# Three changes of buffers in a two-layer decoder: weight pieces loaded a step ahead, projection input placed in the V tiles, query and key stacks as half tiles

## The chip, the cores and the metric

The kernel runs on one core of one Trainium2 chip. The metric is device time in microseconds (us) for one execution of the whole program. A core has five engines with instruction queues of their own: TensorE (PE, matmuls and transposes; its weight loads are listed as PEld), VectorE (DVE), ScalarE (ACT), GpSimd (POOL) and SyncE (SP), which in this kernel issues the DMA transfers. An engine executes its instructions in the order of its queue; between engines, semaphores hold an instruction back until what it needs is there.

## What is computed

The input x has 4 sequences of 1024 tokens and 256 channels, and there is a context of 77 tokens for each sequence. Two pre-LayerNorm layers with residuals follow one another, all in float32:

```
x = x + L0_attn (layernorm(x))            # 16 heads of 16, causal softmax with ALiBi, projection
x = x + L0_xattn(layernorm(x), ctx)       # 16 heads of 64 over the 77 context tokens
x = x + L0_ffn  (layernorm(x))            # BitLinear: silu(gate) * up, then down, inner width 1024
x = x + L1_attn (layernorm(x))            # 16 heads of 16, causal, power attention
x = x + L1_xattn(layernorm(x), ctx)       # 8 heads of 64
x = x + L1_ffn  (layernorm(x))            # FP4: silu(gate) * up, then down, inner width 704
```

The power attention takes weights exp(Z - max Z) with Z = 2 log(|q.k| + 1e-7) + log(scale) + G[t] - G[s], where G is the running sum of log-sigmoid gates that come from 16 extra columns of the same projection. BitLinear rounds weights to three values and activations to 8 bits. The FP4 feed forward rounds weights and activations to the E2M1 grid (0, 0.5, 1, 1.5, 2, 3, 4, 6) with one scale per block of 16 values:

```
scale = max(max|block| / 6, 1e-12)
q     = grid[searchsorted(midpoints, |block / scale|)] * sign * scale
```

## The kernel before

**Precision.** Float32 products are made from a high and a low part of each operand: `split_sb` (ACT copies the high part at L179, DVE subtracts it at L180) and `mm3` (three matmuls, L191). Queries and keys of the attentions are held as three bfloat16 parts, which are laid on top of each other as rows of one contraction.

**Stages.** Sequences are called batches, b = 0 to 3. In phase 0 the layer-0 attention of batch b, `A0(b)`, is the main stream, and the layer-0 cross attention and feed forward of batch b - 1 (`XA(b-1,0)`, `F0(b-1)`) are the side stream; preparations of weights go beside them (`prep_x`, `prep_a1`, `prep_f1_up` beside batch 2, `prep_f1_down` beside batch 3). In phase 1 the layer-1 attention `A1` is the main stream and `XF` (the layer-1 cross attention and feed forward `F1` of the batch before) the side stream; the first side stream is `F0(3)` with what goes before it. After the last main step a tail remains, the cross attention and the feed forward of batch 3, where `F1` runs in several lanes at once, each with its own set of borrowed buffers (the table `FL`, L137 to L142).

**Order.** The streams are Python generators that `weave` and `zip2` interleave by step counts. The framework then orders each engine's instructions by a planner and gives each tile a buffer of its tag. `BUFS` (L128) says how many buffers a tag has; tags that are not listed have one. A tile of a tag has to wait until the last reader of the tile that had the buffer before is done, and its load is then held on SyncE, with whatever is queued behind it. A DMA's issue also waits for the DMA eight issues before it to be complete. PSUM banks are handed out in turn (`BANKS`).

**The front of an attention.** `qkv` (L262 to L307) does a batch in two halves of 512 tokens. `ln` (L215) takes a tile, loads x into it (L223), and normalises: statistics on DVE (L200, L202), a few small steps on GpSimd, and L226 on GpSimd. In phase 0 this tile has the tag "X" (four buffers, shared with the residual's tiles of `load_x`, L167); in phase 1 it is the tag "xn" with one buffer, which the cross attention and the feed forwards use too. A "V" tile is taken next and its padding and its columns of ones are written by GpSimd (L276, L277). The normalised half is transposed by TensorE (L235, tag "Q"), split, multiplied by the weights for queries and keys (results split into bfloat16 parts, L290 to L293, and written to DRAM `dr`, L296 and L297), and for values, which ACT writes into the V tile (L304).

**Stacks.** `stacks` (L310 to L327) brings the parts of four heads back from DRAM: QS by L323 with four DMAs (two sets of parts, two halves of 512 tokens), KS by L320 with two, and in layer 0 the ALiBi rows by L325 and L326. QS and KS have two buffers each, for all 1024 tokens. In layer 0, `a0_max` computes scores on TensorE (L352, and the mask by L356) whose row maxima DVE takes (L357); the negative maxima go back into two rows of QS as a DMA (L386, from a tile VsJ); then `a0_main` multiplies keys by queries again (L401, L403), ACT exponentiates (L404), and TensorE multiplies by V (L413). The next group's `a0_max` is woven with the present group's `a0_main`. In layer 1 the scores are L901, DVE takes them at L907, ACT at L909, GpSimd at L912, and the product with V is L930.

**Weights of the last feed forward.** `prep_f1_up` (L1022 to L1041) does four pieces (w_gate and w_up, two each): it loads a piece into a "wst" tile (two buffers, which all weight preparations share, L1029), rounds it to FP4 in two parts by `fp4` (DVE L1008 to L1011, GpSimd L1012, ACT L1014, DVE L1015 and L1016, GpSimd L1017), transposes it (L1036), splits it and writes it to DRAM `g1d` (L1040). `prep_f1_down` does w_down in two pieces likewise (load L1048, write L1059).

```
    BUFS = {"X": 4, "V": 4, "QS": 2, "KS": 2, "P": 4, "ot": 2, ... "VsJ": 4, "wst": 2, ...}
        for half in range(2):
            xn = self.ln(None, half, src, alt={"xn": "X"} if self.phase == 0 else None)
            V.append(self.t([128, 4, H * 17 + 15], F32, "V"))
```

Of the kernel before, what the change touches and what calls it, by code (L numbers as in the profile page):

```python
# [12 lines left out]
F32 = mybir.dt.float32  # L13
F32R = mybir.dt.float32r
BF = mybir.dt.bfloat16
# [7 lines left out]
B, T, C = 4, 1024, 256  # L23
# [67 lines left out]
class Kern:  # L91
# [13 lines left out]
    def __init__(self, ctx, tc, ins, out, consts, nb=B):  # L105
# [21 lines left out]

    BUFS = {"X": 4, "V": 4, "QS": 2, "KS": 2, "P": 4, "ot": 2, "q4s": 2, "qr": 2, "VsJ": 4, "wst": 2, "E": 2, "kh": 1, "qp": 2, "g_ew": 2}  # L128

# [9 lines left out]
        {"xn": "ot", "xX": "QS", "E": "V", "xph": "y0", "xpl": "y1", "wst": "P", "kh": "KS", "q4s": "VsJ", "ps": 0},  # L139
        {"xn": "DL0", "xX": "QS", "E": "V", "xph": "WAh", "xpl": "WAl", "wst": "P", "kh": "yTh", "q4s": "VsJ", "ps": 1},  # L140
        {"xn": "DL1", "xX": "KS", "E": "V", "xph": "qp", "xpl": "qp", "wst": "P", "kh": "yTl", "q4s": "VsJ", "ps": 1},
    )  # L142
# [72 lines left out]
    def ln(self, b, g, src=None, t0=0, n=4, alt=None):  # L215

        nc = self.nc
        xn = self.t([128, n if alt else 4, C], F32, "xn", alt)[:, :n]
        if src is None:
            x = self.X[b, g][:, t0 : t0 + n]  # L220
        else:
            x = xn
            nc.sync.dma_start(x, src.rearrange("(g t p) c -> g p t c", g=2, p=128)[g])  # L223
# [40 lines left out]
    def qkv(self, src, wd, nw, gl=None, w=None):  # L264
# [7 lines left out]
        for half in range(2):  # L272
            xn = self.ln(None, half, src, alt={"xn": "X"} if self.phase == 0 else None)
            V.append(self.t([128, 4, H * 17 + 15], F32, "V"))
            vv.append(V[half][:, :, 0 : H * 17].rearrange("p t (h e) -> p t h e", e=17))
            nc.gpsimd.memset(V[half][:, :, H * 17 :], 0.0)  # L276
            nc.gpsimd.memset(vv[half][:, :, :, 16:17], 1.0)  # L277
            h = self.t([128, 2, 512], F32R, "yTh")
            l = self.t([128, 2, 512], F32R, "yTl")
            self.xT(xn, h, l, "Q")  # L280
# [29 lines left out]
    def stacks(self, g, dr, alibi):  # L310

        nc = self.nc
        QS = self.t([110, 2, 4, 512], BF, "QS")
        KS = self.t([110, 4, T], BF, "KS")
        c, o = g // 2, (g % 2) * 4
        for st, t0 in ((QS, (1, 0)), (KS, (4, 5))):
            for r in range(2):
                v = dr[c][t0[r] : t0[r] + 3].rearrange("t (d h) n -> (t d) h n", h=8)[:, o : o + 4, :]
                if st is KS:
                    nc.sync.dma_start(KS[r * 48 : r * 48 + 48], v)  # L320
                else:
                    for a in range(2):
                        nc.sync.dma_start(QS[r * 48 : r * 48 + 48, a], v[:, :, a * 512 : a * 512 + 512])  # L323
# [1005 lines left out]
```

## Time and profile before

| | |
|---|---|
| median of three runs | 2400.75 us (2393.45 to 2407.63) |
| the profiled execution | 2399.32 us, of which 2397.5 us are the span of the profile |
| mean granted TensorE clock | 0.953 of full speed |
| TensorE busy | 2149.5 us (90%) |
| VectorE / ScalarE / GpSimd busy | 1698.9 (71%) / 1637.4 (68%) / 1195.4 us (50%) |
| DMA | 238.45 MB in 182,697 packets, mean 99 GB/s |

The shares of busy time are means over stages with different limits, so single stretches are looked at as well. A line of the windows view gives, for a stretch, its length, then the busy time and the number of instructions in brackets of TensorE, weight loads, VectorE, ScalarE and GpSimd, then the granted clock, the share of the DMA engines' time that was used, and the rate in GB/s. A line of the waits view names the engine, the tile and line of the waiting instruction, after the arrow what released it, and then the total, the number and the longest of these waits. The chain of waits follows the work that ended last back through what released it; each piece has its start, its length and what it was.

### The profile page before, as it was taken

What the parts mean: (1) busy time and instruction counts of PE and PEld (TensorE: products, weight loads), DVE (VectorE), ACT (ScalarE), POOL (GpSimd) and SP (SyncE); (2) the same over time, 40 slices, a digit from 0 to 9 for tenths busy, and PEclk for the clock granted to TensorE, in tenths of its full rate; (3) what the DMA queues carried; (4) which work ended last, traced back from release to release, by engine and by line L of the source; (5) the groups of instructions that cost most, each with busy time, mean ns of one, the idle gap of its engine ahead of it and who ended that gap; (6) DMA issues with size and microseconds to landing.
All of it is one profiled execution on the core that took longest, in us unless ns stands there. A gap on an engine that the chain in (4) does not pass through costs nothing.

```text
span 2397.5 us, 51455 instructions
## 1 busy us (share of the span) xinstructions
PE 2149.5 (90%) x19110; PEld 1522.7 (64%) x19110; DVE 1698.9 (71%) x3781; ACT 1637.4 (68%) x4173; POOL 1195.4 (50%) x1942
## 2 busy tenths in 40 slices
PE   6898999998999998999989988899988998898886
PEld 5564557755667754676546765567766776676676
DVE  4776457677766787775756677778767786777776
ACT  4474456676756675665768978887678777888542
POOL 7322212254231442412545457777767787876664
PEclk9898899999999999899989999999999999999897
DMA  8975321223841337312252224412331224442000
GB/s 257 286 193 168 101 72 44 73 64 105 265 105 44 86 95 196 87 44 58 87 174 52 67 70 147 128 39 74 92 104 38 56 88 121 92 98 71 10 10 18
DMA packets 182697, 238.45 MB, mean 99 GB/s; under 512 B 16198, under 2 KB 165846, under 8 KB 175958
## 3 DMA queue, kind: packets, MB, share of 16 engines
q1 hardware_dynamic: 182446, 235.15, 35.5%
q8 instruction: 151, 2.47, 0.4%
q14 instruction: 100, 0.82, 0.1%
HBM read 152.62 MB, written 82.21 MB: 98 GB/s over the span
## 4 chain that ended last, share of the span: by engine, by line
PE 64%; DVE 13%; ACT 8%; DMA 7%; POOL 5%; issue 2%; SPq 1%; DVEq 0%; ACTq 0%; POOLq 0%
PE T L191 11%; PE W L191 9%; PE O L413 7%; PE Q L191 6%; PE O L930 6%; PE S L401 5%; PE M L352 5%; PE S L901 4%; DVE P L907 2%; DVE s_mt L357 2%; PE T L726 2%; PE W L633 1%; ACT P L909 1%; DMA KS<-c_alk 1%; PE M L356 1%
## 5 line engine op out<-in xcount | busy, mean ns | idle before, releaser
L357 DVE TENSOR_REDUCE s_mt<-M 128x1 f32<-128x512 f32 (+3 forms) x608 | 386.1, 655 | 103.9 <-PE M L356 76.2
L404 ACT ACTIVATE P<-S 128x512 f32<-128x512 f32 (+1 forms) x640 | 340.2, 563 | 149.4 <-PE S L401 93.0
L909 ACT ACTIVATE P<-P,eps 128x1024 f32<-128x1024 f32 x320 | 344.6, 1084 | 55.1 <-DVE P L907 52.5
L907 DVE TENSOR_REDUCE P<-S 128x512 f32<-128x512 f32 (+1 forms) x480 | 285.7, 611 | 83.9 <-PE S L901 61.8
L352 PE MATMUL M<-KS,QS 108*128 108x512 bf16 (+3 forms) x768 | 225.6, 339 | 43.3 <-DVE s_mt L357 27.5
L901 PE MATMUL S<-QS,KS 96*128 96x256 bf16 (+1 forms) x1280 | 219.0, 269 | 42.0 <-DVE P L907 35.9
L191 PE MATMUL T<-R,xX 128*128 128x352 f32 (+1 forms) x1136 | 246.8, 332 | 4.9 <-ACT E L622 1.9
L401 PE MATMUL S<-QS,KS 110*128 110x256 bf16 (+1 forms) x1280 | 230.7, 268 | 15.6 <-ACT P L404 8.0
L625 POOL TENSOR_TENSOR E<-E,s_xsm 128x616 f32<-128x616 f32 x64 | 77.8, 1217 | 316.9 <-DVE s_xsm L623 188.3
L413 PE MATMUL O<-P,V 128*32 128x256 f32 (+1 forms) x2560 | 231.4, 374 | 0.1
L191 PEld LDWEIGHTS T<-R,xX 128*128 128x128 f32 x1136 | 183.0, 190 | 25.6 <-ACT E L622 6.5
L912 POOL TENSOR_TENSOR P<-P,y 128x512 f32<-128x512 f32 x128 | 166.5, 1309 | 48.3 <-ACT P L909 28.1
L191 PE MATMUL W<-R,xph 128*128 128x256 f32 (+1 forms) x952 | 184.9, 292 | 3.3 <-ACT xph L179 2.6
L622 ACT ACTIVATE E<-T,s_xmx 128x77 f32<-128x77 f32 x512 | 159.4, 334 | 25.7 <-DVE s_xmx L619 23.0
L930 PE MATMUL O<-P,VsJ 128*32 128x128 f32 x3584 | 171.4, 286 | 5.6 <-ACT P L909 5.3
L901 PEld LDWEIGHTS <-KS 96*128 96x128 bf16 x1280 | 103.9, 99 | 113.4 <-issue 90.6
L401 PEld LDWEIGHTS <-KS 110*128 110x128 bf16 x1280 | 106.4, 100 | 104.9 <-issue 57.2
L191 PEld LDWEIGHTS W<-R,xph 128*128 128x128 f32 (+1 forms) x952 | 149.9, 192 | 12.1 <-issue 3.6
L352 PEld LDWEIGHTS <-QS 108*128 108x128 bf16 x768 | 68.1, 99 | 116.0 <-issue 88.2
L191 PE MATMUL W<-R,xpl 128*128 128x256 f32 (+2 forms) x476 | 139.1, 292 | 1.4 <-DVE xpl L180 1.2
L179 ACT ACTIVATE xph<-W 128x512 fp32r<-128x512 f32 (+2 forms) x180 | 79.6, 459 | 86.6 <-PE W L636 39.6
L733 POOL TENSOR_TENSOR R<-wst 128x256 f32<-128x256 f32 x128 | 92.4, 732 | 83.0 <-DVE wst L732 71.2
(353 smaller groups left out, 5683.8 us busy)
## 6 DMA issues: line engine op xcount, KB each, us to landing
QS<-dr SPq DMA_DIRECT2D x144, 192.0 KB
KS<-dr SPq DMA_DIRECT2D x72, 384.0 KB
dr<-qp SPq DMA_DIRECT2D x32, 768.0 KB
MD<-R SPq DMA_DIRECT2D x24, 616.0 KB
UD<-R SPq DMA_DIRECT2D x24, 512.0 KB
R<-MD SPq DMA_DIRECT2D x32, 308.0 KB
X<-in_x SPq DMA_DIRECT2D x16, 512.0 KB
dr<-qp SPq DMA_DIRECT2D x32, 256.0 KB
```

Source lines behind the costliest of these rows:

```text
L191: nc.tensor.matmul(out, x, y, start=first and n == 0, stop=last and n == len(seq) - 1)
L352: nc.tensor.matmul(Sv[:, x, 0:w], QS[:108, i // 4, hh, i % 4 * 128 : i % 4 * 128 + 128], KS[:108, hh, k0:k1], start=x == 0, stop=not diag ...
L357: nc.vector.tensor_reduce(out, Sv[:, :, 0:w], AX.X, ALU.max)
L401: nc.tensor.matmul(S[:, e, 0:w], st[1][:110, hh, j * 128 : (j + 1) * 128], st[0][:110, q0 // 512, hh, q0 % 512 : q0 % 512 + w], start=e == ...
L404: nc.scalar.activation(P[:, 2 * p : 2 * p + 2, 256 - w :], S[:, :, 0:w], AF.Exp)
L413: nc.tensor.matmul(O[0][hh * 32 : hh * 32 + 32, o + o0 : o + 256], V[j // 4][:, j % 4, h * 17 : h * 17 + 32], P[:, hh, o0:], start=c % 2 = ...
L622: nc.scalar.activation(E[:, n * 77 : (n + 1) * 77], Sv[:, k, :], AF.Exp, bias=mx[:, n : n + 1], accum_out=sm[:, n : n + 1])
L901: nc.tensor.matmul(S[:, e, 0:w], st[r][1][:96, hh, j * 128 : (j + 1) * 128], st[r][0][:96, q0 // 512, hh, q0 % 512 : q0 % 512 + w], start= ...
L907: nc.vector.tensor_reduce(Pv, S[:, :, 0:w].unsqueeze(3), AX.X, ALU.max, apply_absolute_value=True)
L909: nc.scalar.activation(Pw, Pw, AF.Square, bias=self.eps1)
L912: nc.gpsimd.tensor_tensor(Pd, Pd, Ds[r, c][:, j - 2 * c], ALU.mult)
L930: nc.tensor.matmul(Oc[rows, o0 : o0 + 128], lhs, P[:, hh, c0 : c0 + 128], start=j == 2 * c and i == 2 * c, stop=fin and i == 2 * c + 1)
```

## The change

The change has three parts. The computing instructions stay the same in number and shape on every engine.

1. In `prep_f1_up` each piece's load is issued before the piece ahead of it is rounded. The pieces go alternately into a tile of the tag "DU" and one of "wst". In `prep_f1_down` both pieces are loaded at the start.
2. In `qkv`, the two halves of x are loaded straight into the two V tiles at the start of the front, and `ln` normalises them there in place. The writing of V's padding and ones goes behind the transposes that read the normalised values. No "X" or "xn" tile is taken for it any more.
3. `stacks` makes four tiles, QS0, QS1, KS0 and KS1, each with 512 tokens and with two buffers of its own, and loads QS0 and KS0 first, each with its ALiBi rows, then QS1 and KS1. A stack of layer 0 takes 12 DMAs (8 before), one of layer 1 takes 8 (6 before). The users pick the half by the token, and the borrowed buffers of `FL` get the new tags.

```diff
@@ -125,7 +125,7 @@
         self.w1 = None
         self.drn = 0
 
-    BUFS = {"X": 4, "V": 4, "QS": 2, "KS": 2, "P": 4, "ot": 2, "q4s": 2, "qr": 2, "VsJ": 4, "wst": 2, "E": 2, "kh": 1, "qp": 2, "g_ew": 2}
+    BUFS = {"X": 4, "V": 4, "QS0": 2, "QS1": 2, "KS0": 2, "KS1": 2, "P": 4, "ot": 2, "q4s": 2, "qr": 2, "VsJ": 4, "wst": 2, "E": 2, "kh": 1, "qp": 2, "g_ew": 2}
 
 
     BANKS = (
@@ -136,9 +136,9 @@
     XL = {"xX": "yTh", "R2": "yTl", "M0": "WAh", "M1": "WAl", "U0": "qp", "U1": "qp", "E": "V", "xph": "qr", "xpl": "qr"}
     FL = (
         None,
-        {"xn": "ot", "xX": "QS", "E": "V", "xph": "y0", "xpl": "y1", "wst": "P", "kh": "KS", "q4s": "VsJ", "ps": 0},
-        {"xn": "DL0", "xX": "QS", "E": "V", "xph": "WAh", "xpl": "WAl", "wst": "P", "kh": "yTh", "q4s": "VsJ", "ps": 1},
-        {"xn": "DL1", "xX": "KS", "E": "V", "xph": "qp", "xpl": "qp", "wst": "P", "kh": "yTl", "q4s": "VsJ", "ps": 1},
+        {"xn": "ot", "xX": "QS0", "E": "V", "xph": "y0", "xpl": "y1", "wst": "P", "kh": "KS0", "q4s": "VsJ", "ps": 0},
+        {"xn": "DL0", "xX": "QS1", "E": "V", "xph": "WAh", "xpl": "WAl", "wst": "P", "kh": "yTh", "q4s": "VsJ", "ps": 1},
+        {"xn": "DL1", "xX": "KS1", "E": "V", "xph": "qp", "xpl": "qp", "wst": "P", "kh": "yTl", "q4s": "VsJ", "ps": 1},
     )
 
     @staticmethod
@@ -215,12 +215,11 @@
     def ln(self, b, g, src=None, t0=0, n=4, alt=None):
 
         nc = self.nc
-        xn = self.t([128, n if alt else 4, C], F32, "xn", alt)[:, :n]
         if src is None:
+            xn = self.t([128, n if alt else 4, C], F32, "xn", alt)[:, :n]
             x = self.X[b, g][:, t0 : t0 + n]
         else:
-            x = xn
-            nc.sync.dma_start(x, src.rearrange("(g t p) c -> g p t c", g=2, p=128)[g])
+            x = xn = src
         rs, mb = self.stats(x)
         for i in range(n):
             nc.gpsimd.tensor_scalar(xn[:, i, :], x[:, i, :], mb[:, i : i + 1], rs[:, i : i + 1], ALU.add, ALU.mult)
@@ -270,14 +269,16 @@
             self.n += 1
             dr.append(self.dr.tile([8, 128, T], BF, tag=f"dr{c}", name=f"dr{c}_{self.n}", bufs=2))
         for half in range(2):
-            xn = self.ln(None, half, src, alt={"xn": "X"} if self.phase == 0 else None)
             V.append(self.t([128, 4, H * 17 + 15], F32, "V"))
+            nc.sync.dma_start(V[half][:, :, :C], src.rearrange("(g t p) c -> g p t c", g=2, p=128)[half])
+        for half in range(2):
+            xn = self.ln(None, half, V[half][:, :, :C])
+            h = self.t([128, 2, 512], F32R, "yTh")
+            l = self.t([128, 2, 512], F32R, "yTl")
+            self.xT(xn, h, l, "Q")
             vv.append(V[half][:, :, 0 : H * 17].rearrange("p t (h e) -> p t h e", e=17))
             nc.gpsimd.memset(V[half][:, :, H * 17 :], 0.0)
             nc.gpsimd.memset(vv[half][:, :, :, 16:17], 1.0)
-            h = self.t([128, 2, 512], F32R, "yTh")
-            l = self.t([128, 2, 512], F32R, "yTl")
-            self.xT(xn, h, l, "Q")
             yield
             hs = slice(half * 512, (half + 1) * 512)
             for c in range(2):
@@ -310,20 +311,19 @@
     def stacks(self, g, dr, alibi):
 
         nc = self.nc
-        QS = self.t([110, 2, 4, 512], BF, "QS")
-        KS = self.t([110, 4, T], BF, "KS")
+        QS, KS = [], []
         c, o = g // 2, (g % 2) * 4
-        for st, t0 in ((QS, (1, 0)), (KS, (4, 5))):
-            for r in range(2):
-                v = dr[c][t0[r] : t0[r] + 3].rearrange("t (d h) n -> (t d) h n", h=8)[:, o : o + 4, :]
-                if st is KS:
-                    nc.sync.dma_start(KS[r * 48 : r * 48 + 48], v)
-                else:
-                    for a in range(2):
-                        nc.sync.dma_start(QS[r * 48 : r * 48 + 48, a], v[:, :, a * 512 : a * 512 + 512])
-        if alibi:
-            nc.sync.dma_start(QS[96:108], self.c["alq"][:, g])
-            nc.sync.dma_start(KS[96:110], self.c["alk"][:, g * 4 : g * 4 + 4, :])
+        for a in range(2):
+            n = slice(a * 512, a * 512 + 512)
+            for st, nm, t0 in ((QS, "QS", (1, 0)), (KS, "KS", (4, 5))):
+                t = self.t([110, 4, 512], BF, f"{nm}{a}")
+                st.append(t)
+                for r in range(2):
+                    v = dr[c][t0[r] : t0[r] + 3].rearrange("t (d h) n -> (t d) h n", h=8)[:, o : o + 4, n]
+                    nc.sync.dma_start(t[r * 48 : r * 48 + 48], v)
+            if alibi:
+                nc.sync.dma_start(QS[a][96:108], self.c["alq"][:, g, a])
+                nc.sync.dma_start(KS[a][96:110], self.c["alk"][:, g * 4 : g * 4 + 4, n])
         return QS, KS
 
 
@@ -349,7 +349,7 @@
             st_ = 512 // n
             Sv = S.rearrange("p (n k) -> p n k", n=n)
             for x, (hh, i, k0, k1) in enumerate(pieces):
-                nc.tensor.matmul(Sv[:, x, 0:w], QS[:108, i // 4, hh, i % 4 * 128 : i % 4 * 128 + 128], KS[:108, hh, k0:k1], start=x == 0, stop=not diag and x == n - 1)
+                nc.tensor.matmul(Sv[:, x, 0:w], QS[i // 4][:108, hh, i % 4 * 128 : i % 4 * 128 + 128], KS[k0 // 512][:108, hh, k0 % 512 : k0 % 512 + w], start=x == 0, stop=not diag and x == n - 1)
             if diag:
                 r = self.maskb if n == 1 else self.maskb.unsqueeze(1).to_broadcast([128, n, 128])
                 o = Sv[:, 0, w - 128 : w] if n == 1 else Sv[:, :, w - 128 : w]
@@ -383,7 +383,7 @@
         nc.scalar.activation(pr[:, 0, :], ps[:16, :128], AF.Copy)
         nc.vector.tensor_tensor(pr[:, 1, :], ps[:16, :128], pr[:, 0, :], ALU.subtract)
         for p in range(2):
-            nc.sync.dma_start(st[0][108 + p : 109 + p, part].rearrange("o h (i n) -> o (h i) n", n=128), pr[:, p, :])
+            nc.sync.dma_start(st[0][part][108 + p : 109 + p].rearrange("o h (i n) -> o (h i) n", n=128), pr[:, p, :])
 
     def a0_main(self, st, V, y, g, O, pend):
         nc = self.nc
@@ -398,7 +398,7 @@
                 S = self.p("S").rearrange("p (h k) -> p h k", h=2)
                 for e in range(2):
                     hh = 2 * p + e
-                    nc.tensor.matmul(S[:, e, 0:w], st[1][:110, hh, j * 128 : (j + 1) * 128], st[0][:110, q0 // 512, hh, q0 % 512 : q0 % 512 + w], start=e == 0, stop=not dg and e == 1)
+                    nc.tensor.matmul(S[:, e, 0:w], st[1][j // 4][:110, hh, j % 4 * 128 : j % 4 * 128 + 128], st[0][q0 // 512][:110, hh, q0 % 512 : q0 % 512 + w], start=e == 0, stop=not dg and e == 1)
                 if dg:
                     nc.tensor.matmul(S[:, :, 0:128], self.identb, self.maskTb.unsqueeze(1).to_broadcast([128, 2, 128]), start=False, stop=True)
                 nc.scalar.activation(P[:, 2 * p : 2 * p + 2, 256 - w :], S[:, :, 0:w], AF.Exp)
@@ -898,7 +898,7 @@
                 S = self.p("S").rearrange("p (h k) -> p h k", h=2)
                 for e in range(2):
                     hh = 2 * p + e
-                    nc.tensor.matmul(S[:, e, 0:w], st[r][1][:96, hh, j * 128 : (j + 1) * 128], st[r][0][:96, q0 // 512, hh, q0 % 512 : q0 % 512 + w], start=e == 0, stop=e == 1)
+                    nc.tensor.matmul(S[:, e, 0:w], st[r][1][j // 4][:96, hh, j % 4 * 128 : j % 4 * 128 + 128], st[r][0][q0 // 512][:96, hh, q0 % 512 : q0 % 512 + w], start=e == 0, stop=e == 1)
                 Pv = P[:, 2 * p : 2 * p + 2, 256 - w :]
                 self.absn += 1
                 if self.absn % 8 in ABS_ACT:
@@ -1022,11 +1022,19 @@
     def prep_f1_up(self):
         nc = self.nc
         self.g1d = self.dr.tile([2, 128, 2, 2, 2, 352], F32, name="g1d")
-        for n, nm in enumerate(("w_gate", "w_up")):
-            src = self.i["L1_ffn_" + nm].rearrange("(t p) k -> p t k", p=88)
+        sts = []
+
+        def load(n, t2):
+            src = self.i["L1_ffn_" + ("w_gate", "w_up")[n]].rearrange("(t p) k -> p t k", p=88)
+            sts.append(self.t([128, 1024], F32, "DU" if t2 == 0 else "wst")[:88])
+            nc.sync.dma_start(sts[-1].rearrange("p (t k) -> p t k", k=256), src[:, t2 * 4 : t2 * 4 + 4, :])
+
+        load(0, 0)
+        for n in range(2):
             for t2 in range(2):
-                st = self.t([128, 1024], F32, "wst")[:88]
-                nc.sync.dma_start(st.rearrange("p (t k) -> p t k", k=256), src[:, t2 * 4 : t2 * 4 + 4, :])
+                st = sts.pop()
+                if (n, t2) != (1, 1):
+                    load(n + t2, 1 - t2)
                 for k in range(2):
                     self.fp4(st[:, k * 512 : (k + 1) * 512], 32, 1e-12)
                 yield
@@ -1043,9 +1051,12 @@
     def prep_f1_down(self):
         nc = self.nc
         self.d1d = self.dr.tile([128, 2, 6, 256], F32, name="d1d")
+        sts = []
         for r in range(2):
-            st = self.t([128, 1024], F32, "wst")[:, :704]
-            nc.sync.dma_start(st[:, 0:704], self.i["L1_ffn_w_down"][r * 128 : (r + 1) * 128, :])
+            sts.append(self.t([128, 1024], F32, "wst")[:, :704])
+            nc.sync.dma_start(sts[r], self.i["L1_ffn_w_down"][r * 128 : (r + 1) * 128, :])
+        for r in range(2):
+            st = sts[r]
             self.fp4(st[:, 0:704], 44, 1e-12)
             for c2 in range(3):
                 ps = self.p("T")
```

## The prediction

> **What bounds the kernel now.** I read the shares of the engines first, then the windows, the waits of each engine, and the chain of waits around the places that the diff touches.
>
> ```profile
> span 2397.5 us, 51455 instructions
> ...
> PE 2149.5 (90%) x19110; PEld 1522.7 (64%) x19110; DVE 1698.9 (71%) x3781; ACT 1637.4 (68%) x4173; POOL 1195.4 (50%) x1942
> ...
> PE 64%; DVE 13%; ACT 8%; DMA 7%; POOL 5%; issue 2%; SPq 1%; DVEq 0%; ACTq 0%; POOLq 0%
> ```
>
> TensorE is the bound, and it is idle for 2397.5 - 2149.5 = 248 us. The change has the same compute instructions on every engine (the two programs' counts agree), so it can only move idle time and clock. The profiled run took 2399.3 us, 1.4 below the median of 2400.75; the sum is made against 2399.3.
>
> Windows by stage (columns: PE, weight loads, DVE, ACT, POOL busy, granted clock, DMA share, GB/s):
>
> ```profile
> 60.00:120.00 60.00, 49.29 (x270) 33.09 (x270) 45.35 (x84) 26.19 (x60) 18.75 (x17) 0.86 0.95 287
> ...
> 900.00:960.00 60.00, 48.43 (x391) 24.20 (x390) 43.92 (x94) 33.10 (x64) 12.85 (x18) 0.91 0.74 196
> ```
> ```profile
> 170.00:180.00 10.00, 5.42 (x49) 3.52 (x48) 6.04 (x12) 4.08 (x9) 0.00 (x0) 0.86 1.05 230
> 180.00:190.00 10.00, 8.75 (x74) 4.89 (x75) 5.58 (x14) 4.16 (x9) 3.72 (x3) 0.80 0.82 255
> 190.00:200.00 10.00, 6.61 (x27) 2.77 (x26) 5.46 (x10) 1.68 (x3) 1.12 (x2) 0.55 1.01 336
> ```
> ```profile
> 2200.00:2245.30 45.30, 40.66 (x496) 27.56 (x496) 36.19 (x77) 35.44 (x52) 28.57 (x51) 0.96 0.04 14
> 2245.30:2397.50 152.20, 114.75 (x710) 105.66 (x710) 101.92 (x201) 56.55 (x163) 89.36 (x104) 0.85 0.03 11
> ```
>
> TensorE has its holes where a stack of queries and keys or a weight arrives late (170 to 200, 900 to 960), with a lower granted clock behind each hole, and in the tail behind the last L901, which starts at 2245.3. Waits of TensorE, then of VectorE (total us, times, longest):
>
> ```profile
> PE M L352 <- DMA KS<-c_alk: 6.4, 4, 2.6
> ...
> PE M L352 <- DMA MD<-R: 5.2, 1, 5.2
> ```
> ```profile
> DVE q4s L1008 <- DMA wst<-in_L_ffn_w_up: 7.1, 2, 6.1
> ```
>
> The 5.2 is named after a weight's round trip, but the first max matmul (L352) reads only the stack, whose last load (L326) is issued at 171.45, 0.8 us before that transfer: I count it to the stack. The chain (start, us, what):
>
> ```profile
> 172.22 8.44 DMA MD<-R
> ...
> 224.47 8.06 DMA KS<-c_alk
> ```
> ```profile
> 941.80 12.35 DMA wst<-in_L_ffn_w_up
> ...
> 961.65 4.84 DMA wst<-in_L_ffn_w_up
> ```
> ```profile
> 1407.57 5.80 DMA xn<-xs
> ```
>
> **The change part by part.**
>
> *Stacks in halves.* A stack of layer 0 becomes 12 DMAs instead of 8 (16 stacks), one of layer 1 8 instead of 6 (20 stacks): 64 + 40 = 104 more issues. SyncE spends about 0.43 us on one (L323), so 104 x 0.43 = 45 us of a queue, spread over 36 places, beside other work; the bytes are the same. The gain: the first half (QS0, KS0) is complete after 6 issues rather than 8, and its buffers come free with the last score matmul (L401) on the lower half, earlier than the whole tile. By the old trace's times of the releasing instructions, KS0's load can go at 155.1 instead of 167.9, 214.4 instead of 220.1, about 372 instead of 386, while the first L352 of the stack keeps its place in TensorE's order. A transfer of 8.1 to 8.4 us (chain) then lands before that place. So the two wait rows go: 6.4 + 5.2 = 11.6 us. Behind the 5.2 us hole the clock was 0.80 over 8.75 busy us, which is 1.75 us lost, most of it the hole's: 13.4. What is late next is the augmented row QS<-VsJ (chain: 6.41 us from 189.29), which the change leaves. TensorE is the bound 90% of the time: I take 0.9 x 13.4 = -12. Bounds: nothing (the wait passes to QS<-VsJ) and -16 (the 0.55 clock of 190 to 200 gets better too, 3.0 us).
>
> The Trainium skill's "DMA: Bandwidth & Descriptors", section "Bandwidth", tells to batch transfers to 1 MiB and more, and "Anatomy of one DMA" gives each about 2.0 us of fixed cost, which speaks against this part. Row against rule: with transfers of 192 to 384 KB the old trace moves 336 GB/s at 190 to 200. By the page, 104 x 2.0 = 208 us, of which the DMA share of the chain (7%) would be +15 (an estimate) and the whole sum about -2. The runs decide.
>
> *Weights one step ahead.* The 6.07 us wait of VectorE at 948 (load issued at 941.80, landed 954.2) left TensorE idle for 4.86 us at 955.6, since the max reductions L357 stand behind L1008; a second, 4.84 us in the chain, leaves 2.42 us at 968.4. Now each piece is loaded while the one before is rounded. I take the 4.86 and some 60% of the 2.42 as gone: -6.3. Added: the second piece of w_gate is now loaded into "wst" at about 917.6, when the buffer comes free, and lands 5 to 7 us later, while VectorE's L1008 on it stands right behind an L180 that ended at 919.9. That is a wait of 2.5 to 5 us, again with L357s queued behind it, and TensorE waits for those; priced as before (4.86 / 6.07 = 0.8), +2 to +4. I take +2.8. Net -3.5; bounds -8 (all three holes of 955 to 970 go: 4.9 + 1.6 + 2.4 = 8.9, less a bit) and +2 (the new wait at 5 us, and a second at the first piece of w_up, which goes to "DU" behind another DU load and lands about when it is read). The first piece of w_gate is quantised at about 645 instead of 930; the same 4.6 us of VectorE, beside the same kind of attention. w_down's waits (2.8 us) fall to about 1, covered by TensorE's other streams; nothing taken.
>
> *Input into V.* In phase 0, x goes to V as soon as V is free, not to a rotating X buffer: at the start, six loads of 512 KB stand in a row on SyncE instead of three. 1.5 MB at 287 GB/s is 5 us in front of the weights and of dr, in a stage where DMA is at 0.95. On the other side, the first max units move forward in TensorE's order (first L352 from place 263 to 131), and fill holes of a stage that is idle 10.7 of 60 us; they can stand in order before their stack has landed, though. Ends: -7.8 (the chain's "QS<-dr" at 71.72 goes) and +5; nothing favours one, so the middle, -1.4. VectorE and GpSimd: the memsets of L276/L277 only move behind the transposes, 2 of POOL's 1,947 instructions per half, engine 50% busy; nothing, and should POOL be late there, under 1 us a front.
>
> In phase 1 the single "xn" is no longer shared by the fronts of the next batch with the feed forward and the cross attention. The load at 1407.57 came when L710 let go of xn; TensorE then waited 2.30 us at 1421.9, and 3.77 us at 1849.5 after the like load at 1839.2. I take half of these 6.1: -3. Bounds 0 (V tiles also serve E of the cross attention, whose release takes the place of xn's) and -14 (both loads out of the chain, 5.8 + 8.5).
>
> *The tail.* The main stream of phase 1 no longer waits, so the woven side work falls behind it: the last main matmul (L930) moves from place 14,871 to 14,759 of 15,517, and 112 matmuls of the side streams go behind it. Spread in the stream they cost about 0.21 us each (T and W by L191: 246.8 / 1136, 184.9 / 952), 23.5 us taken off before the end; behind it, the tail's 644 took 152.2 us, 0.236 each: +26.4. Net +3; bounds 0 and +26 (the main stream ends no earlier).
>
> Sum: -12 - 3.5 - 1.4 - 3 + 3 = -17: 2399.3 - 17 = 2382.
>
> On the clock: the Trainium skill's "TensorE: Matmul & The Clock Gate", Part 1, has half speed for about 3.4 us after an idle window. The trace's row is milder behind the 5.2 us hole (0.80 over 10 us), so 1.75 us; the page would make 1.7 of it, and the sum the same.
>
> **The rivals.**
>
> *A. The side work lands on the tail (slower).* In the new order the side is 30 to 35 us of main-stream time late at 2200. If the main stream gets no faster for it, because its pace is set by P's chain (waits of L901 for L907, 35.9 us) and not by TensorE's load, then these 33 us come behind 2245 and the front's gain is none: -12 - 3.5 - 1.4 + 33 = +16, 2415. It decides when the last L930 starts no earlier than before (2250). For it: 152 us of tail at clock 0.85. Against: PE 40.66 of 45.3 busy before it. 0.22.
>
> *B. The weights' wait only moves.* Weights +2, the rest as forecast: 2388. For it: the load at 917.6. 0.12.
>
> *C. The stack holes change owner.* The QS<-VsJ row or L357 ends the wait: stacks 0, sum -5, 2394. For it: the 6.41 us of that transfer right behind. Against: it belongs to another step. 0.12.
>
> *D. A jam at the start.* +5 and the first L352 waiting in order another 5: 2399.3 - 17 + 11 = 2394. 0.06.
>
> *E. All of it.* Stacks -16, weights -8, fronts -14, tail +3, start -1.4: 2363. For it: the clock, which rises with every hole that goes. 0.13.
>
> **How the numbers follow.** The forecast has 0.35. About 0.5% (12 us) is what a measurement of this kernel can tell from no change. Faster: most of the forecast and E (0.43), half of B and a little of C: 0.55. Same: the rest of B, C and D and the edge of the forecast: 0.22. Slower: A at its price, and more than one term at its bad end: 0.23. The forecast's own range is 2370 to 2394. The 8 in 10 range goes from under E (2345) to A with the jam added (2420).
>
> **What would show it.** Right: no wait of L352 for KS or MD rows above 1 us; windows 170 to 240 near 55 of 60 busy at clock 0.95; L1008's longest wait below 3 us; the last L930 starting by about 2215 and a tail near 175 us. Wrong: L1008 waiting at 920 for over 5 us; QS1 or KS1 as new releasers of L352; the last L930 at 2245 with a tail of 175; DMA above 0.95 past 130 us.

## The result and the profile after

The changed kernel takes 2405.5 us (median of 21 runs) against 2399.85 of before (21 runs): ratio 1.0029, interval 1.0018 to 1.0040. It is slower by some 6 us, inside the 0.5% that the forecast called no change, and it was forecast faster, at 2382. The profiled execution of after took 2404.46 us.

The page of the changed kernel, shares of the engines, the chain, and the packets of DMA:

```profile
span 2402.6 us, 51558 instructions
...
PE 2152.9 (90%) x19072; PEld 1531.1 (64%) x19110; DVE 1693.3 (70%) x3781; ACT 1636.5 (68%) x4173; POOL 1195.5 (50%) x1942
...
DMA packets 210218, 238.46 MB, mean 99 GB/s; under 512 B 17766, under 2 KB 196854, under 8 KB 207350
...
q1 hardware_dynamic: 209966, 235.16, 34.1%
...
PE 59%; DVE 16%; POOL 8%; ACT 7%; DMA 7%; issue 3%; SPq 1%; ACTq 0%; POOLq 0%; DVEq 0%
```

TensorE is as busy as before. Most of the waits that the forecast wanted to remove are gone, though. The windows that had holes, changed kernel (length, then busy time of PE, weight loads, DVE, ACT, POOL, granted clock, DMA share, GB/s):

```profile
60.00:120.00 60.00, 54.36 (x343) 36.93 (x343) 46.34 (x88) 32.60 (x75) 21.44 (x21) 0.91 0.88 275
900.00:960.00 60.00, 48.84 (x405) 25.61 (x406) 48.75 (x108) 34.22 (x68) 14.92 (x18) 0.90 0.82 240
170.00:180.00 10.00, 9.38 (x80) 5.82 (x78) 6.64 (x15) 6.06 (x14) 0.00 (x0) 1.00 0.71 227
180.00:190.00 10.00, 9.05 (x88) 5.00 (x89) 8.28 (x16) 6.27 (x12) 4.31 (x4) 1.00 0.99 271
190.00:200.00 10.00, 10.00 (x100) 4.97 (x100) 7.61 (x13) 6.81 (x14) 0.00 (x0) 1.00 0.87 279
```

From 170 to 200 TensorE was busy for 20.8 us at clocks down to 0.55; it is now busy for 28.4 at 1.00. Part of that is lost again just behind: from 200 to 240 it is busy for 33.7 us at 0.87, before for 35.1 at 0.97. And from 900 to 960 it is hardly fuller than before (48.8 against 48.4 us), although the longest wait for a weight there has fallen from 6.1 to 1.1 us. The waits of TensorE on transfers, changed kernel:

```profile
PE D L873 <- DMA DL<-locd: 15.8, 7, 6.8
PE S L401 <- DMA QS<-VsJ: 7.0, 6, 2.0
PE M L352 <- DMA KS<-dr: 0.8, 1, 0.8
```

The 11.6 us of L352 behind the stacks' last loads are down to about 1 us. A new row leads: the layer-1 gates' reload (2.6 us before).

So where did it go? I cut both executions at two points, the end of the last L413 (end of phase 0) and of the last L930 (end of the main stream). Windows of before, then of after:

```profile
0.00:1263.20 1263.20, 1144.65 (x9008) 747.41 (x9008) 865.98 (x1912) 785.79 (x2182) 426.68 (x623) 0.96 0.44 124
1263.20:2251.00 987.80, 893.01 (x9434) 671.29 (x9433) 735.53 (x1678) 797.86 (x1833) 682.13 (x1217) 0.96 0.31 82
2251.00:2397.50 146.50, 111.83 (x670) 104.00 (x670) 97.39 (x194) 53.78 (x159) 86.59 (x102) 0.85 0.03 12
```
```profile
0.00:1244.40 1244.40, 1139.94 (x8987) 750.14 (x9014) 864.91 (x1913) 785.64 (x2188) 426.33 (x622) 0.96 0.43 127
1244.40:2230.90 986.50, 886.84 (x9331) 663.86 (x9339) 717.28 (x1655) 789.28 (x1813) 674.64 (x1210) 0.96 0.29 80
2230.90:2402.60 171.70, 126.14 (x759) 117.06 (x758) 111.14 (x215) 61.53 (x174) 94.55 (x110) 0.85 0.04 13
```

Phase 0 is 18.8 us shorter, with as many matmuls in it but for six (9,008 and 9,014 weight loads; the matmul column lacks some records). Phase 1 is 1.3 us shorter, although it does 94 matmuls less by its weight loads. The tail that does them instead is 25.2 us longer. The sum is +5.1. (From the last L930 on, that one counted in, 671 matmuls stood in TensorE's order before and 759 do now, so 88 have moved. The forecast's 112 was counted from the stream's last transpose, L943, behind which 644 stood and 756 do now.)

### The profile page after: what moved, and what is told of

The parts are those of the page before. It is cut to its first block, busy times and chain, and to the rows that moved or that the text cites. A ratio compares the mean times of both kernels' runs of the same rounds, so it can differ in the third digit from the quotient of the medians.

```text
span 2402.6 us, 51558 instructions
## 1 busy us (share of the span) xinstructions
PE 2152.9 (90%) x19072; PEld 1531.1 (64%) x19110; DVE 1693.3 (70%) x3781; ACT 1636.5 (68%) x4173; POOL 1195.5 (50%) x1942
## 2 busy tenths in 40 slices
DMA packets 210218, 238.46 MB, mean 99 GB/s; under 512 B 17766, under 2 KB 196854, under 8 KB 207350
## 3 DMA queue, kind: packets, MB, share of 16 engines
q1 hardware_dynamic: 209966, 235.16, 34.1%
## 4 chain that ended last, share of the span: by engine, by line
PE 59%; DVE 16%; POOL 8%; ACT 7%; DMA 7%; issue 3%; SPq 1%; ACTq 0%; POOLq 0%; DVEq 0%
PE T L191 10%; PE W L191 8%; PE O L413 7%; PE Q L191 5%; PE S L401 5%; PE O L930 5%; PE M L352 4%; PE S L901 3%; DVE P L907 2%; DVE s_mt L357 2%; POOL P L912 2%; PE W L633 1%; PE T L726 1%; DMA DL<-locd 1%; PE M L356 1%
## 5 line engine op out<-in xcount | busy, mean ns | idle before, releaser
L352 PE MATMUL M<-KS,QS 108*128 108x512 bf16 (+3 forms) x768 | 223.9, 337 | 31.7 <-DVE s_mt L357 25.2
L191 PE MATMUL T<-R,xX 128*128 128x352 f32 (+1 forms) x1136 | 245.8, 332 | 5.7 <-DVE wst L1109 1.9
L401 PE MATMUL S<-QS,KS 110*128 110x256 bf16 (+1 forms) x1280 | 228.5, 266 | 14.7 <-DMA QS<-VsJ 7.0
L413 PE MATMUL O<-P,V 128*32 128x256 f32 (+1 forms) x2560 | 226.4, 372 | 0.1
L191 PEld LDWEIGHTS T<-R,xX 128*128 128x128 f32 x1136 | 183.1, 190 | 27.3 <-ACT E L622 5.8
L191 PE MATMUL W<-R,xph 128*128 128x256 f32 (+1 forms) x952 | 186.3, 293 | 4.4 <-DVE xpl L180 3.6
L930 PE MATMUL O<-P,VsJ 128*32 128x128 f32 x3584 | 177.1, 284 | 4.9 <-ACT P L909 4.0
L401 PEld LDWEIGHTS <-KS 110*128 110x128 bf16 x1280 | 106.8, 99 | 100.8 <-issue 52.2
L191 PEld LDWEIGHTS W<-R,xph 128*128 128x128 f32 (+1 forms) x952 | 150.5, 193 | 13.1 <-DVE xpl L180 4.2
L191 PE MATMUL W<-R,xpl 128*128 128x256 f32 (+2 forms) x476 | 139.8, 294 | 1.1 <-DVE xpl L180 0.9
L930 PEld LDWEIGHTS O<-P,VsJ 128*32 128x32 f32 x3584 | 102.7, 112 | 47.2 <-issue 29.2
L352 PEld LDWEIGHTS <-QS 108*128 108x128 bf16 x768 | 67.4, 99 | 102.3 <-issue 82.3
```

Of the source, the lines that this page charges most:

```text
L191: nc.tensor.matmul(out, x, y, start=first and n == 0, stop=last and n == len(seq) - 1)
L352: nc.tensor.matmul(Sv[:, x, 0:w], QS[i // 4][:108, hh, i % 4 * 128 : i % 4 * 128 + 128], KS[k0 // 512][:108, hh, k0 % 512 : k0 % 512 + w], ...
L401: nc.tensor.matmul(S[:, e, 0:w], st[1][j // 4][:110, hh, j % 4 * 128 : j % 4 * 128 + 128], st[0][q0 // 512][:110, hh, q0 % 512 : q0 % 512 ...
L413: nc.tensor.matmul(O[0][hh * 32 : hh * 32 + 32, o + o0 : o + 256], V[j // 4][:, j % 4, h * 17 : h * 17 + 32], P[:, hh, o0:], start=c % 2 = ...
L930: nc.tensor.matmul(Oc[rows, o0 : o0 + 128], lhs, P[:, hh, c0 : c0 + 128], start=j == 2 * c and i == 2 * c, stop=fin and i == 2 * c + 1)
```

## The experiments

All fourteen, with these three stretches of the profiled execution. "Behind" is the number of matmuls that the order has from the last L930 on. Ratios are to executions of the kernel before that were taken together with the run; their medians lie between 2395.65 and 2399.85, so that ratios compare better across rows than medians do.

| run | median us | ratio (interval) | phase 0 | phase 1 | tail | phase 1 + tail | behind |
|---|---|---|---|---|---|---|---|
| before | 2399.85 | 1 | 1263.2 | 987.8 | 146.5 | 1134.3 | 671 |
| the change | 2405.5 | 1.0029 (1.0018 to 1.0040) | 1244.4 | 986.5 | 171.7 | 1158.2 | 759 |
| e1 halves | 2378.62 | 0.9917 (0.9897 to 0.9937) | 1245.9 | 988.5 | 142.3 | 1130.8 | 671 |
| e2 V input | 2387.74 | 0.9955 (0.9942 to 0.9968) | 1255.8 | 970.1 | 156.6 | 1126.7 | 755 |
| e3 weights | 2405.58 | 1.0036 (1.0021 to 1.0052) | 1251.7 | 1011.5 | 135.9 | 1147.4 | 587 |
| e4 halves + weights | 2386.36 | 0.9950 (0.9932 to 0.9968) | 1238.2 | 998.5 | 138.6 | 1137.1 | 665 |
| e5 halves + V | 2400.66 | 1.0014 (1.0000 to 1.0028) | 1245.1 | 986.7 | 163.4 | 1150.1 | 755 |
| e6 weights + V | 2400.72 | 1.0027 (1.0017 to 1.0038) | 1250.8 | 982.9 | 158.6 | 1141.5 | 749 |
| e7 halves + V in phase 0 | 2399.1 | 1.0004 (0.9991 to 1.0018) | 1241.7 | 1013.7 | 139.0 | 1152.7 | 581 |
| e8 halves + V in phase 1 | 2392.08 | 0.9971 (0.9953 to 0.9989) | 1243.2 | 987.2 | 162.3 | 1149.5 | 755 |
| e9 e5, side at 78 | 2378.65 | 0.9917 (0.9897 to 0.9937) | 1240.0 | 984.8 | 146.1 | 1130.9 | 671 |
| e10 e1, side at 78 | 2427.6 | 1.0119 (1.0100 to 1.0139) | 1238.5 | 1047.9 | 134.5 | 1182.4 | 587 |
| e11 the change, side at 78 | 2380.48 | 0.9928 (0.9908 to 0.9949) | 1245.3 | 988.5 | 140.9 | 1129.4 | 671 |
| e12 weights, side at 62 | 2389.71 | 0.9959 (0.9945 to 0.9974) | 1259.5 | 996.4 | 139.6 | 1136.0 | 677 |
| e13 V input, side at 78 | 2389.07 | 0.9953 (0.9937 to 0.9970) | 1258.2 | 990.2 | 139.4 | 1129.6 | 641 |
| e14 e7, side at 62 | 2384.82 | 0.9941 (0.9925 to 0.9957) | 1243.6 | 997.0 | 141.7 | 1138.7 | 671 |

### The three parts, alone and in pairs

**e1**, the halves alone (the hunks of `BUFS`, `FL`, `stacks` and the users of the stacks):

```diff
-        QS = self.t([110, 2, 4, 512], BF, "QS")
-        KS = self.t([110, 4, T], BF, "KS")
+        for a in range(2):
+            for st, nm, t0 in ((QS, "QS", (1, 0)), (KS, "KS", (4, 5))):
+                t = self.t([110, 4, 512], BF, f"{nm}{a}")
```

> Only the half tiles of queries and keys; weights and V input as before. Theory 1 (the V input alone makes the tail longer; the halves' gain in phase 0 is real): the KS and MD waits of L352 (11.6 us) go, the last L413 starts 10 to 14 us before 1262.9, the tail behind the last L930 stays at about 147 us, and the time is 2386 to 2391. Theory 2 (whatever speeds the main stream only moves side work to the end): the last L930 is 10 us or more earlier, the tail 10 us or more longer, and the time is 2397 to 2403.

Measured: 2378.62, 18.5 us less than before (2397.09 in the same set). Both theories were too high, theory 1 by less: of the 20.8 us that this execution is shorter, 17.3 are in phase 0, and the tail is not longer. Cut as above:

```profile
0.00:1245.90 1245.90, 1137.91 (x8983) 747.65 (x9008) 867.90 (x1912) 785.68 (x2182) 425.91 (x623) 0.95 0.43 126
1245.90:2234.40 988.50, 890.97 (x9425) 675.08 (x9433) 725.94 (x1677) 796.25 (x1832) 680.06 (x1217) 0.97 0.29 81
2234.40:2376.70 142.30, 107.45 (x670) 99.52 (x670) 97.45 (x194) 53.74 (x160) 86.75 (x103) 0.89 0.04 12
```

**e2**, the V input alone (the hunks of `ln` and `qkv`):

```diff
-            xn = self.ln(None, half, src, alt={"xn": "X"} if self.phase == 0 else None)
+            nc.sync.dma_start(V[half][:, :, :C], src.rearrange("(g t p) c -> g p t c", g=2, p=128)[half])
+        for half in range(2):
+            xn = self.ln(None, half, V[half][:, :, :C])
```

> Only the input loaded into V tiles. Theory 1: the tail behind the last L930 grows from 147 to about 170 us, since 84 more matmuls stand behind it in the order, the main stream of phase 1 takes as long as before, and the time is 2405 to 2420 (worse than the whole change, which has the halves' gain). Theory 2: the tail grows only with the main stream's own gain; 2395 to 2403.

Measured: 2387.74, below both theories. The tail did grow, to 156.6, but phase 1 fell by 17.7. Alone, this part behaves as the forecast had it for the whole:

```profile
1255.80:2225.90 970.10, 877.95 (x9333) 660.88 (x9344) 715.56 (x1657) 789.42 (x1815) 676.67 (x1211) 0.97 0.31 82
2225.90:2382.50 156.60, 120.54 (x758) 112.15 (x754) 107.83 (x213) 60.02 (x173) 92.11 (x109) 0.88 0.04 14
```

**e3**, the weights alone (the hunks of `prep_f1_up` and `prep_f1_down`):

```diff
-                st = self.t([128, 1024], F32, "wst")[:88]
-                nc.sync.dma_start(st.rearrange("p (t k) -> p t k", k=256), src[:, t2 * 4 : t2 * 4 + 4, :])
+                st = sts.pop()
+                if (n, t2) != (1, 1):
+                    load(n + t2, 1 - t2)
```

> Only the weights' loads a step ahead. Theory 1: the 6 us wait of L1008 at 948 goes, one of about 4 us comes at 640, where the first piece of w_gate is now read 3 us after its load is issued in a full DMA stage; phase 0 is 0 to 4 us shorter. In the order 84 matmuls move from behind the last L930 to before it, which takes some 15 us off the tail and puts them in the main stream: 2393 to 2401. Theory 2: 2399 to 2403, with the main stream later and the tail shorter by the same amount.

Measured: 2405.58, slower than before and above both ranges. Theory 1's wait is there (waits of VectorE, e3):

```profile
DVE q4s L1008 <- DMA DU<-in_L_ffn_w_gate: 4.2, 1, 4.2
```

Phase 0 is still 11.5 us shorter in this execution; the loss is in phase 1, which is 23.7 us longer, while the tail is only 10.6 us shorter.

**e4**, the change without the hunks of `ln` and `qkv`:

```diff
-            xn = self.ln(None, half, V[half][:, :, :C])
+            xn = self.ln(None, half, src, alt={"xn": "X"} if self.phase == 0 else None)
```

> The whole change without the V input: halves and weights. Theory 1: both gains of phase 0, a tail of about 147 us: 2381 to 2390, faster than both kernels. Theory 2: 2397 to 2404.

Measured: 2386.36, as theory 1 said. The ratios of e1 and e3 multiply to 0.9953, and 0.9950 was measured: in time, these two parts add up. (In the order they don't: 665 matmuls are behind here, 671 with the halves and 587 with the weights.)

**e5 and e6** undo the weights or the halves in the whole change (the diffs of e3 and e1, reversed).

```diff
-                    load(n + t2, 1 - t2)
+                st = self.t([128, 1024], F32, "wst")[:88]
```

> The whole change without the weights a step ahead: halves and V input. Alone, the halves gave -18.5 us, the V input -9.4, the weights +8.5, together -19.4; the whole change measured +6, so some 25 us come from two or three parts meeting. Theory 3 (halves and V input get in each other's way in phase 1: the loads of the halves wait on SyncE in front of the loads of the gates DL<-locd, and the side work lands in the tail): 2390 to 2400, with DL<-locd waits of L873 above 8 us and a tail of about 165 us. Theory 4 (the weights' part upsets phase 1 where it meets another part): 2366 to 2375, A1 at about 970 us and a tail of 150.

> The whole change without the halves: weights a step ahead and V input. Theory 3: the sum of the two parts, 2392 to 2399, with short DL<-locd waits and a tail of about 153 us. Theory 4: 2402 to 2415, a phase 1 and a tail as long as with the whole change (986 and 168 us).

Measured: 2400.66 and 2400.72. From the single parts, 0.9872 and 0.9991 would follow; measured were 1.0014 and 1.0027. So the V input loses with each of the others, most with the halves: some 34 us (1.4%). Theory 3 has the time of e5 nearly right, but its cause falls: in e5 no wait of L873 for DL<-locd is over 1 us. Theory 4 falls with e5 (2366 to 2375 were expected), and e6 lies between the ranges of the two. In e5 phase 1 is as long as before, and the tail is long:

```profile
1245.10:2231.80 986.70, 887.93 (x9332) 661.51 (x9344) 724.70 (x1658) 793.17 (x1814) 678.57 (x1211) 0.96 0.28 80
2231.80:2395.20 163.40, 121.76 (x758) 113.79 (x754) 110.70 (x212) 60.25 (x172) 96.36 (x109) 0.86 0.04 14
```

### Where the parts meet

**e7 and e8** take the halves with the V input in one phase only.

```diff
+        inV = self.phase == 0        # 1 in e8
...
+            if inV:
+                xn = self.ln(None, half, x=V[half][:, :, :C])
+            else:
+                xn = self.ln(None, half, src, alt={"xn": "X"} if self.phase == 0 else None)
```

> Halves, and the V input in phase 0 alone (phase 1's fronts use xn as before). Halves and V input together measured 2400.7, where their single gains would give some 2368: about 33 us are lost where they meet, by the traces about 7 in phase 0, 16 in phase 1 and 11 in the tail. Theory 5 (the meeting place is phase 1: the fronts that no longer wait for xn let the main stream run ahead of the side work, which is then done late, alone and in the tail): 2374 to 2384, like the halves alone, with phase 0 ending at about 1245. Theory 6 (the V input harms where phase 0 is concerned, by moving loads at the start): 2390 or more, phase 0 ending later than 1250.

> Halves, and the V input in phase 1 alone. Theory 5: 2392 to 2402, phase 0 ending at about 1246, a tail of about 160 us. Theory 6: 2360 to 2372, since phase 1 then keeps the 17 us that the V input alone gained there.

Measured: 2399.1 and 2392.08. e8 is at the lower edge of theory 5. e7 has theory 6's time, and not its reason: phase 0 ended at 1241.7, early. Its phase 1 is 25 us longer than e1's, with no change to phase 1's code, and here 581 matmuls stand behind the last L930, not 671. This pointed at the order itself. 587, 671 and 755 are 84 apart. The matmuls in between belong to batch 2's last feed forward (L191 on T and W, and their transposes): two portions of 84, one after the other, of which the planner puts none, the second, or both behind the main stream's end. What stands behind of them is called the late group below.

**e9 and e10** change one step count, that of the weaves of batches 1 and 2 (batch 0 keeps 85, and the weave of batch 3, in which the late group stands, keeps its counts). The late group moves by way of the planner, and not alone: from about 1550 to 1720 us on, some 4,800 to 6,400 of TensorE's 19,110 matmuls stand in other places in the kernels with another step count, by up to 341 places; before that the orders agree. So these runs test the order of the side work as a whole; no run moves the group by itself.

```diff
-                run_all(weave(main, 96, side, 85 if b == 0 else 68))
+                run_all(weave(main, 96, side, 85 if b == 0 else 78))
```

> Halves and V input, and the side streams of batches 0 to 2 woven in at 78 steps to the main stream's 96 instead of 68, so that in the order 671 matmuls stand behind the last L930, as many as before, instead of 755. Theory 5 (the delayed side work is what costs): a tail of 140 to 147 us, phase 1 at about 985 and the time 2378 to 2388. If the tail falls by 15 us and phase 1 grows by as much, 2398 to 2403: then the tail is only where the loss shows.

> The halves alone with the same 78 for 68 (587 matmuls behind the last L930 instead of 671). A control: theory 5 has nothing late to repair, so the tail falls by 7 to 10 us, phase 1 grows by as much, and the time stays within 5 us of the halves alone (2374 to 2384). Theory 7 (phase 1 is a matter of luck of the order, and any reshuffle moves it by 10 us and more): outside of that, either way.

Measured: e9 2378.65, 22 us less than e5, as theory 5 said; phase 1 didn't grow for the 84 matmuls that it took back, and the tail fell by 17.3:

```profile
1240.00:2224.80 984.80, 889.35 (x9417) 666.91 (x9427) 726.48 (x1676) 794.56 (x1828) 683.68 (x1218) 0.97 0.29 81
2224.80:2370.90 146.10, 109.17 (x672) 101.71 (x670) 97.12 (x194) 53.73 (x160) 88.01 (x103) 0.86 0.03 12
```

The control e10 did not stay: 2427.6, 49 us more than e1. Its phase 1 has a wait that is 1.2 us in e1 (waits of TensorE, e10):

```profile
PE T L235 <- POOL xn L1016: 22.1, 6, 9.4
```

This suggests that here the feed forward's and the fronts' uses of the single "xn" queue behind each other, so that the earlier side runs into the buffer that the V input frees: with the V input and 78 steps the same row is 4.3 (e9), 1.3 (e11) and 2.6 us (e13). So theory 7's letter was met; some 21 of the 49 us have a name, the rest has none.

**e11 to e14** change the step count in the whole change (78, the line of e9), in the weights alone (62), the V input alone (78) and e7 (62).

```diff
-                run_all(weave(main, 96, side, 85 if b == 0 else 68))
+                run_all(weave(main, 96, side, 85 if b == 0 else 62))
```

> The whole change with 78 steps for 68 in the weaving of batches 0 to 2, which puts 671 matmuls behind the last L930 instead of 759. Theory 5 (the late block): phase 0 ends at 1244 as before, phase 1 takes about 985 us and the tail 142 to 148: 2375 to 2386. If the parts themselves cost phase 1: phase 1 at 1000 or more, 2393 to 2405.

> The weights alone with 62 steps for 68, which puts 677 matmuls behind the last L930 instead of 587. Theory 5: phase 0 ends at about 1252 as with the weights alone, phase 1 falls from 1011 to about 990 and the tail grows to 143: 2384 to 2392, faster than before. If the weights' part itself upsets phase 1: 2400 to 2410.

> The V input alone with 78 steps for 68, which puts 641 matmuls behind the last L930 instead of 755. By the prices of the forecast (0.21 us in the stream, 0.236 behind it) 114 matmuls move for a gain of 3 us: phase 1 at 994, tail at 140, 2382 to 2389. Theory 5 with a cost of the late block here too: 2370 to 2380.

> Halves and the V input in phase 0 alone, with 62 steps for 68: 671 matmuls behind the last L930 instead of 581. Theory 5: phase 0 ends at about 1242, phase 1 falls from 1014 to about 988, the tail grows to 142: 2372 to 2382. If not: 2394 to 2404 again.

Measured: 2380.48, 2389.71, 2389.07, 2384.82. e11, e12 and e14 fell by 25.0, 15.9 and 14.3 us (e14 ends 3 above its range); the first two are where theory 5 put them. e13 stayed at its forecast by prices (upper edge), and within 2 us of e2: in the V input alone the late group cost nothing. e11, cut as above:

```profile
0.00:1245.30 1245.30, 1140.74 (x8987) 748.42 (x9014) 865.86 (x1913) 786.00 (x2189) 426.48 (x622) 0.96 0.43 126
1245.30:2233.80 988.50, 895.33 (x9417) 670.81 (x9427) 724.03 (x1676) 795.86 (x1828) 683.71 (x1218) 0.97 0.29 80
2233.80:2374.70 140.90, 104.84 (x672) 97.03 (x670) 96.27 (x194) 53.84 (x160) 85.26 (x103) 0.92 0.04 12
```

With 641 to 677 matmuls behind the last L930, phase 1 and tail take 1129 to 1139 us together in all eight such kernels, whichever parts they have. With both portions late (749 to 759) it is 1141 to 1158 in four, and with none (581 to 587) 1147 to 1182 in three. The one exception is e2, the V input alone, with both portions late and 1126.7. Why it costs nothing there, and does as soon as the halves or the weights are added, stays open. The six pairs of kernels that differ in the step count alone show what the matmuls behind the last L930 cost, each figure from two single profiles:

| pair | more matmuls behind | phase 1 | tail |
|---|---|---|---|
| e3 to e12 | 90 | -15.1 | +3.7 |
| e7 to e14 | 90 | -16.7 | +2.7 |
| e10 to e1 | 84 | -59.4 | +7.8 |
| e13 to e2 | 114 | -20.1 | +17.2 |
| e9 to e5 | 84 | +1.9 | +17.3 |
| e11 to the change | 88 | -2.0 | +30.8 |

So it isn't simply bad to be late. The first portion that goes behind takes some 15 us or more off phase 1 and adds 3 to 8 us to the tail. The second adds 17 to 31 us to the tail, and phase 1 gives nothing for it where the halves are in. Two rivals are left. Theory 7, that any other order moves phase 1 by such amounts, isn't refuted, because thousands of places change in each pair and e10 and e2 fit no rule. And the kernel before wasn't run with 62 or 78 steps, so the ratios of e9 and of e11 to e14 contain what the step count alone would have given.

## Why the prediction was wrong

**Phase 0 came out right as a whole, by luck: its shares weren't.** The forecast took -12 (stacks), -3.5 (weights) and -1.4 (start), -17 in all; phase 0 became 18.8 us shorter. Alone, the halves take 17.3 (e1) and 24.7 us (e10, the same phase 0), the weights 11.5 and 3.7 (e3, e12), the V input 7.4 and 5.0 (e2, e13). They don't add up: with all three, 18.8 and 17.9 (e11). All of these are against the one profile of before.

- *Stacks.* Right, and too small: the loads go early enough, L352's waits for them go, and the clock behind them rises, as the windows from 170 to 200 show (with the halves alone, e1, TensorE is busy for 28.4 us there at 1.00 too). The forecast's two prices of the clock behind the old hole, 1.75 and 1.7 us, are the same, so that row wasn't the milder one. The estimate from the page "DMA: Bandwidth & Descriptors" of the Trainium skill, section "Anatomy of one DMA", +15 us for 104 more transfers, is not seen: with the -12 it would make this part a loss of 3 us, and e1 gained 18.5. The page gives its 2.0 us for DMAs that GpSimd issues; here SyncE issues them. What the transfers cost by themselves no run shows. The packets rose from 182,697 to 210,218 and the share of DMA time in the queue fell from 35.5% to 34.1%.
- *Weights.* The two old waits went, and the new wait was put at the wrong piece. "The same 4.6 us of VectorE, beside the same kind of attention" left out the load: the first piece of w_gate is issued at 633.61, where DMA is full (a share of 1.06 from 633 to 641), and read at once. The waiting line of VectorE, changed kernel, with its idle time before it in brackets:

```profile
640.65 1.28 DVE L1008 TENSOR_REDUCE q4s<-DU 88x32 f32<-88x512 f32 x2 [4.08 <-DMA DU<-in_L_ffn_w_gate]
```

  The second piece, which I priced at 2.5 to 5 us, waited 1.1. That this part shortens phase 0 is right by the 11.5 and 3.7 us above, within their error; as a whole the weights alone are slower (1.0036, e3), because of phase 1, and faster with 62 steps (0.9959, e12).
- *Input into V, start.* Within its ends, by the 7.4 and 5.0 us above. The first L401 starts at 105.6 instead of 109.3 with the V input alone (e2), at 103.0 with the halves alone (e1), and at 96.2 with all three.

**Phase 1 and the tail are the step that failed.** "Spread in the stream they cost about 0.21 us each ... 23.5 us taken off before the end; behind it ... 0.236 each: +26.4. Net +3." With the -3 of the fronts, phase 1 and tail were to take as long as before; they took 23.9 us longer (1158.2 against 1134.3). The basis was off first: 88 matmuls moved behind the last L930, not 112, and the 152.2 us of the old tail hold 710 matmuls, not 644, by the window from 2245.30. But that makes the prices 0.21 on both sides and the net still about nothing. What failed is that what goes behind is saved in front. The whole change and e11 differ by 88 matmuls: phase 1 is 988.5 - 986.5 = 2.0 us shorter without them, where 18 were priced, and the tail is 171.7 - 140.9 = 30.8 us longer with them, 0.35 each. I priced a matmul in the stream by TensorE's busy time, as if TensorE's load set the pace of phase 1. In this pair and in e9 and e5 it does not: TensorE's busy time in phase 1 falls from 895.33 to 886.84 us, and its idle time grows by 6.5. In the pairs e3 and e12, e7 and e14, e13 and e2 phase 1 did give 0.17 to 0.19 us a matmul, so the price isn't wrong everywhere. Which engine sets the pace where it fails was not tested.

**Fronts.** -3 was taken for the loads that no longer wait for "xn". The waits did go: TensorE's 2.3 us for "xn" in a front (L235, tag "Q") and VectorE's 4.7 us at L200 for the loads of "xn" are in no row of the changed kernel. Phase 1 fell by 1.3 us with 94 matmuls less, so no gain can be told. The loads into V now wait 18.2 us on SyncE for L636, the cross attention's last reader of such a buffer, as the forecast's bound of 0 had it, and the rows of DL<-locd (15.8 us against 2.6) are new; with 8.3 us of them e11 is fast, so they don't explain the loss. In e11, with 671 behind as before, phase 1 takes 988.5 against 987.8.

**Rival A says what happened**, with the point of decision misplaced: the main stream of phase 1 got no faster (986.5 against 987.8), and the work came behind it. Its reason, that P's chain sets the pace, was not tested. But I had it decide by the last L930 at 2250, which phase 0's gain moved to 2230.5 by itself; what it should have asked is the length of phase 1. Its price of 33 us was 25, and its 2415 was 2405.5.

## What to carry to other kernels

A gain in one stage is worth what the stages behind it let through: before a total is given, the places of the side work in every engine's order have to be compared, and a piece that falls behind the main stream's end can be paid in the tail without being saved in the stream (88 matmuls: 30.8 us against 2.0). A busy share of 90% doesn't say that removing work from a stream shortens it. And when a change of buffers reshuffles an order, it is the change and the interleaving that have to be tuned together: the same change was 0.3% slower at 68 steps and 0.7% faster at 78, and the halves alone do as well without it.

## What was unexpected

- One phase 0 program, in two executions: 1245.9 and 1238.5 (e1, e10), 1251.7 and 1259.5 (e3, e12), 1245.1 and 1240.0 (e5, e9), 1244.4 and 1245.3 (the change, e11). Stretches of single profiles are good to about 8 us here, no better.
- Twice as many KS transfers at half the size, with rows of half the length, left DMA's busy share no higher (34.1% against 35.5%) and its bytes the same.
- The V input, in phase 0 alone, changed the order of phase 1, whose code it doesn't touch, and made it 25 us longer (e7 against e1).
